# The head of a fused attention and mixture-of-experts kernel: order of the first loads, inverse roots of the first blocks on GpSimd, place of the router's centring, and the first slot tile's step

## The chip, the cores and the metric

The kernel runs on one core of one Trainium2 chip. A core has TensorE (PE, matrix products, with a weight load PEld ahead of each), VectorE (DVE), ScalarE (ACT), GpSimd (POOL) and SyncE (SP, which here only issues DMAs). Each engine works through its own instructions in order; they meet at semaphores. ScalarE, SyncE and GpSimd each have a queue for DMAs. The metric is the device time of one execution in microseconds.

## The reference

x is 4 sequences of 2048 rows of 256 numbers, all in float32.

```python
x = x + linear_attention(layernorm(x))     # 16 heads of 16
x = x + moe(layernorm(x))                  # 8 experts, 2 a row, 256 -> 512 -> 256
# linear attention, causal, with q, k = elu(...) + 1:
#   S_t = S_{t-1} + k_t v_t^T;  z_t = z_{t-1} + k_t
#   out_t = (q_t S_t) / (q_t z_t + 1e-6), then times Wo
# moe: logits = x router^T; the two largest, softmax over those two;
#   sum over them of p * (gelu(x w1 + b1) w2 + b2)
```

## The kernel before, in words

**Blocks.** The 8192 rows go through attention in 16 blocks of 512 rows (four tiles of 128). A block passes three stages, one a round of the main loop (L946): `stage_a` (L364: normalised rows transposed, keys, queries, running sum z of the keys, values with the router's eight columns, transposed keys, denominators), `stage_b` (L465: scores of each 128 rows, mask, products with the values, state), `stage_c` (L562: output projection px, x1 = x + attention, x1 stored to the output, choice of two experts, second normalising, slot of each row, and eight scatters L659 on GpSimd's queue that write each row twice to a table in DRAM, sorted by expert). In round s the loop runs stage a of block s, b of s-1 and c of s-2, a piece of each in turn.

**Slot tiles.** The table is worked off in 68 tiles of 256 rows of one expert (`slot_tiles`, L767), and up to four more under a condition. `plan` (L673) chooses the experts of a group of tiles (of 5, 4, 8, 8, 8, 8, 8 and 22) once the blocks that it needs are scattered. A tile is: fetch of its rows (L782, which waits for every scatter issued before it in the program), of w1 (L794), of w2 and b2 (L802, L806); `turned` (TensorE transposes, L815, copied by VectorE, L816); `hidden` (ph, L843, and Gelu on ScalarE); `output` (py, L860, plus b2 and weighted on VectorE, L865 and L869); and two indirect stores with addition into the output (L874, GpSimd's queue), each pair after the pair before it and after all x1 stores issued before it. The generator yields twice a tile: after hidden(j), turned(j+1) and the fetches of rows j+3 and w1 j+2; and after output(j-1), the store of an earlier tile and the fetch of w2 j+1. The main loop puts such steps between the pieces of attention by count (L955 to L972); ten steps are kept back for the last round, the rest follows when attention is over.

**Order.** SP's instructions stand in the order of the program (L108, written by hand). On the other engines a scheduler orders them by its own estimate of when they are ready. DMA semaphores are eight, handed out in turn, so a later DMA may have to wait for an earlier one that has the same semaphore.

**The head.** Block 0's rows come in four loads of 128 KB on ScalarE's queue (L120); the four 256 KB weights wk, wq, wv, wo on SP's (L131); then, on ScalarE's, the biases (L140 to L146), the router (L148) and b1 (L150). GpSimd builds the identity, masks and zeroed buffers (L154 to L217). `enter` (L354) normalises a block: statistics on VectorE (L271, L272), variance plus epsilon (L274), an inverse root by a bit trick and three Newton steps, eleven operations on 128x4 (L277 to L287), std and shift (L289, L292), then two of the four tiles normalised on VectorE (L302) and two on ScalarE (L297); GpSimd adds the output bias to x (L359). For blocks 1 to 5 it is called in stage a of the block before (L429); later blocks call it in their own stage a. `centre_router` (L318) takes the mean of the router's rows off (two matmuls with ones, two VectorE operations L326 that write eight columns beside wv); it is called in stage a of block 0, just ahead of the values.

Of the kernel before, what the change touches and what calls it, by code (L numbers as in the profile page):

```python
# [16 lines left out]
P = 128  # L17
# [7 lines left out]
def kernel(  # L25
# [89 lines left out]
    def load_x(n: int):  # L115
        b, s0 = blocks[n]
        xt = att.tile([P, NT, D], F32, tag="x", bufs=4, name=f"x_{n}")
        step = P if n == 0 else TB
        for i in range(0, TB, step):
            nc.scalar.dma_start(  # L120
                xt[:, i // P : (i + step) // P, :],
                x[b, s0 + i : s0 + i + step, :].rearrange("(t p) d -> p t d", p=P),
            )
        return xt
# [4 lines left out]
    def load_square(w, name, more=0):  # L129
        t = wpool.tile([P, NCC, D + more], F32, tag=name, name=name)  # L130
        nc.sync.dma_start(t[:, :, 0:D], w.rearrange("(cc p) o -> p cc o", p=P))  # L131
        return t

    wk_sb = load_square(wk, "wk_sb")
    wq_sb = load_square(wq, "wq_sb")

    wv_sb = load_square(wv, "wv_sb", E)
    wo_sb = load_square(wo, "wo_sb", E)
    bq_sb = const.tile([P, NCC], F32, tag="bq", name="bq_sb")
    nc.scalar.dma_start(bq_sb, bq)  # L140
    bk_sb = const.tile([P, NCC], F32, tag="bk", name="bk_sb")
    nc.scalar.dma_start(bk_sb, bk)
    bv_bc = const.tile([P, D], F32, tag="bv", name="bv_bc")
    nc.scalar.dma_start(bv_bc, bv.partition_broadcast(P))
    bo_bc = const.tile([P, D], F32, tag="bo", name="bo_bc")
    nc.scalar.dma_start(bo_bc, bo.partition_broadcast(P))  # L146
    rw_sb = const.tile([P, NCC, E], F32, tag="rw", name="rw_sb")
    nc.scalar.dma_start(rw_sb, rw.rearrange("(cc p) e -> p cc e", p=P))  # L148
    b1_sb = const.tile([P, E * NFC], F32, tag="b1", name="b1_sb")
    nc.scalar.dma_start(b1_sb, b1)  # L150
# [3 lines left out]
    make_identity(nc, ident)  # L154
    causal = const.tile([P, P], F32, tag="causal", name="causal")
# [68 lines left out]
    def ins_of(i):  # L224
        return getattr(i, "ins", i)

# [8 lines left out]

    def follow(inst, other):

        tc.add_manual_dep(
            ins_of(inst), ins_of(other).name,
            mybir.DependencyInfo(  # L240
                mybir.DependencyClass.NoSync, mybir.DependencyReason.SCHED_ONLY
            ), reason="order of issue",
        )
# [21 lines left out]

    def layernorm(src, dst, root_of=None):

        st = small.tile([P, NT, 6], F32, tag="st", name="st")
        mv = small.tile([P, NT, 2], F32, tag="mv", name="mv")
        for t in range(NT):  # L270
            nc.vector.bn_stats(st[:, t, :], src[:, t, :])  # L271
            nc.vector.bn_aggr(mv[:, t, :], st[:, t, :])  # L272
        rstd = small.tile([P, NT], F32, tag="rstd", name="rstd")
        nc.vector.tensor_scalar_add(rstd, mv[:, :, 1], LN_EPS)  # L274

        half = small.tile([P, NT], I32, tag="half", name="half")
        nc.vector.tensor_single_scalar(  # L277
            half, rstd.bitcast(I32), 1, op=ALU.logical_shift_right
        )
        guess = small.tile([P, NT], I32, tag="guess", name="guess")  # L280
        nc.vector.tensor_scalar(guess, half, -1.0, float(0x5F3759DF), ALU.mult, ALU.add)
        root = guess.bitcast(F32)
        error = small.tile([P, NT], F32, tag="error", name="error")
        for _ in range(3):
            nc.vector.scalar_tensor_tensor(error, root, -0.5, root, ALU.mult, ALU.mult)
            nc.vector.tensor_tensor(error, error, rstd, ALU.mult)
            nc.vector.scalar_tensor_tensor(root, error, 1.5, root, ALU.add, ALU.mult)  # L287
        if root_of is not None:
            nc.vector.tensor_tensor(root_of, rstd, root, ALU.mult)  # L289
        rstd = root  # L290
        shift = small.tile([P, NT], F32, tag="shift", name="shift")
        nc.vector.scalar_tensor_tensor(  # L292
            shift, mv[:, :, 0], -1.0, rstd, ALU.mult, ALU.mult
        )
        for t in range(NT):
            if t % 2:
                nc.scalar.activation(  # L297
                    dst[:, t, :], src[:, t, :], AF.Identity,
                    bias=shift[:, t : t + 1], scale=rstd[:, t : t + 1],
                )  # L300
                continue
            nc.vector.tensor_scalar(  # L302
                dst[:, t, :], src[:, t, :], mv[:, t, 0:1], rstd[:, t : t + 1],
                ALU.subtract, ALU.mult,
            )
        return rstd
# [45 lines left out]
    entered = {}  # L352

    def enter(n: int):  # L354
        xt = xs.pop(n)
        xn = att.tile([P, NT, D], F32, tag="xn", bufs=2, name=f"xn_{n}")
        std = small.tile([P, NT], F32, tag="std", bufs=3, name=f"std_{n}")
        layernorm(xt, xn, std)
        nc.gpsimd.tensor_tensor(  # L359
            xt, xt, bo_bc.unsqueeze(1).to_broadcast([P, NT, D]), ALU.add  # L360
        )
        entered[n] = xt, xn, std
# [668 lines left out]
```

## Time and profile before

| | |
|---|---|
| time, median of 3 runs | 1098.58 us (1096.32 to 1100.79) |
| profiled execution, its own time | 1100.39 us |
| its span, first to last instruction | 1098.5 us |
| mean granted TensorE clock | 0.968 |
| TensorE busy | 1005.2 us (92%) |
| VectorE busy | 763.7 us (70%) |
| ScalarE busy | 406.7 us (37%) |
| GpSimd busy | 387.0 us (35%) |
| chain that ended last, by engine | PE 69%, DVE 20%, DMA 6%, waiting for nothing shown 3% |

The profile is of one execution. A busy share is a mean over stretches with different limits, so it has to be read by stretch: which engine is full there, and what ended the idle time of the others. In timelines a row gives the start, the time taken, the engine, the line, the operation, output and inputs, the count, and in brackets the idle time before it with what ended that. A queue's name with a q (SPq, ACTq) marks an instruction that issues a DMA.

### The profile page before, as it was taken

What the parts mean: (1) busy time and instruction counts of PE and PEld (TensorE: products, weight loads), DVE (VectorE), ACT (ScalarE), POOL (GpSimd) and SP (SyncE); (2) the same over time, 40 slices, a digit from 0 to 9 for tenths busy, and PEclk for the clock granted to TensorE, in tenths of its full rate; (3) what the DMA queues carried; (4) which work ended last, traced back from release to release, by engine and by line L of the source; (5) the groups of instructions that cost most, each with busy time, mean ns of one, the idle gap of its engine ahead of it and who ended that gap; (6) DMA issues with size and microseconds to landing.
All of it is one profiled execution on the core that took longest, in us unless ns stands there. A gap on an engine that the chain in (4) does not pass through costs nothing.

```text
span 1098.5 us, 23167 instructions
## 1 busy us (share of the span) xinstructions
PE 1005.2 (92%) x8358; PEld 802.0 (73%) x8358; DVE 763.7 (70%) x2665; ACT 406.7 (37%) x842; POOL 387.0 (35%) x302
## 2 busy tenths in 40 slices
PE   4998888789998999999999999999999879999991
PEld 2666565576767787878787877788788768888880
DVE  8877989769797769795979688767776713343320
ACT  3543343424452535353535344363532112222220
POOL 4003123022342424435353525153325343444344
PEclk9998998889999999999999999999999989999996
DMA  6001123342525474655647382837374588999853
GB/s 213 1 21 60 42 68 119 113 145 49 175 49 175 92 217 97 189 136 151 178 102 220 76 251 59 233 60 215 82 217 107 159 247 231 227 238 242 229 129 39
DMA packets 128724, 155.23 MB, mean 141 GB/s; under 512 B 9952, under 2 KB 105952, under 8 KB 128608
## 3 DMA queue, kind: packets, MB, share of 16 engines
q1 hardware_dynamic: 84944, 101.78, 29.4%
q0 software_dynamic: 25728, 34.88, 17.3%
q10 hardware_dynamic: 17936, 17.07, 4.9%
q8 instruction: 67, 1.10, 0.4%
q14 instruction: 49, 0.40, 0.1%
HBM read 108.05 MB, written 45.65 MB: 140 GB/s over the span
## 4 chain that ended last, share of the span: by engine, by line
PE 69%; DVE 20%; DMA 6%; issue 3%; POOL 1%; ACT 1%; ACTq 0%; POOLq 0%; SPq 0%; DVEq 0%
PE py L860 19%; PE ph L843 18%; PE pp L381 6%; PE pn L514 5%; DMA out_dram<-y,to 5%; PE sc L486 4%; DVE at L491 4%; PE pv L406 4%; PE px L574 4%; PE pn L507 3%; PE pt_xs L815 2%; DVE st L271 2%; DVE z L391 2%; PE pt_xn L263 1%; PE pk L425 1%
## 5 line engine op out<-in xcount | busy, mean ns | idle before, releaser
L874 POOL DMA_INDIRECT out_dram<-y,to x136 | 216.6, 1592 | 459.4 <-DVE y L869 112.9
L843 PE MATMUL ph<-xT,w 128*128 128x256 f32 x1088 | 253.8, 387 | 13.4 <-DMA w<-in_w_dram 7.6
L860 PE MATMUL py<-w,hT 128*128 128x256 f32 x1088 | 250.9, 384 | 0.0
L843 PEld LDWEIGHTS ph<-xT,w 128*128 128x128 f32 x1088 | 208.6, 194 | 45.5 <-issue 15.6
L860 PEld LDWEIGHTS py<-w,hT 128*128 128x128 f32 x1088 | 202.8, 191 | 32.8 <-issue 4.7
L849 ACT ACTIVATE hT<-ph,b1t 128x256 f32<-128x256 f32 x272 | 112.4, 471 | 301.5 <-PE ph L843 261.5
L491 DVE TENSOR_TENSOR at<-sc,causal 128x512 f32<-128x512 f32 x256 | 158.4, 682 | 8.9 <-PE sc L486 8.9
L659 POOL DMA_INDIRECT rows<-xn,slots x128 | 124.5, 973 | 49.4 <-issue 33.2
L865 DVE TENSOR_TENSOR y<-py,b 128x512 f32<-128x512 f32 x68 | 46.9, 690 | 124.2 <-PE py L860 124.2
L816 DVE COPY xT<-pt_xs 128x512 f32<-128x512 f32 x68 | 46.8, 689 | 98.8 <-PE pt_xs L815 98.8
L359 POOL TENSOR_TENSOR x<-x,bo_bc 128x1024 f32<-128x1024 f32 x16 | 37.8, 2361 | 196.6 <-ACT xn L297 138.4
L477 ACT ACTIVATE qM<-qs,parity 128x256 f32<-128x256 f32 x128 | 56.3, 499 | 93.2 <-DVE qs L456 44.2
L486 PE MATMUL sc<-qM,kT 32*128 32x256 f32 x1024 | 76.0, 401 | 5.7 <-ACT share L416 5.3
L514 PE MATMUL pn<-at,vpad 128*32 128x128 f32 x2048 | 74.0, 288 | 0.0
L486 PEld LDWEIGHTS sc<-qM,kT 32*128 32x128 f32 x1024 | 47.6, 184 | 32.0 <-issue 16.9
L406 PE MATMUL pv<-wv_sb,xnT 128*128 128x264 f32 x256 | 62.9, 399 | 8.6 <-DVE wv_sb L326 4.8
L514 PEld LDWEIGHTS pn<-at,vpad 128*32 128x32 f32 x2048 | 55.3, 115 | 8.8 <-issue 1.1
L406 PEld LDWEIGHTS pv<-wv_sb,xnT 128*128 128x128 f32 x256 | 48.4, 195 | 17.8 <-DVE wv_sb L326 4.9
L574 PE MATMUL px<-wo_sb,vT 128*128 128x264 f32 x256 | 61.1, 392 | 0.0
L869 DVE TENSOR_SCALAR y<-y,wt 128x256 f32<-128x256 f32 x136 | 58.5, 472 | 1.9
L381 PE MATMUL pp<-xnT,wk_sb 128*128 128x512 f32 x128 | 59.6, 609 | 0.2 <-ACT xnT L264 0.2
L381 PE MATMUL pp<-xnT,wq_sb 128*128 128x512 f32 x128 | 58.2, 597 | 0.0
(163 smaller groups left out, 1288.1 us busy)
## 6 DMA issues: line engine op xcount, KB each, us to landing
w<-in_w_dram SPq DMA_DIRECT2D x136, 512.0 KB, 5.7
xs<-rows SPq DMA_DIRECT2D x68, 260.0 KB, 3.3
b<-in_b_dram SPq DMA_DIRECT2D x68, 128.0 KB, 5.8
out_dram<-x ACTq DMA_DIRECT2D x16, 512.0 KB, 4.5
x<-in_x_dram ACTq DMA_DIRECT2D x15, 512.0 KB, 4.3
rows<-none SPq DMA_DIRECT2D x1, 2340.0 KB, 9.4
out_dram<-y,to POOLq DMA_INDIRECT x136, 3.9
rows<-xn,slots POOLq DMA_INDIRECT x128, 2.5
```

The lines of the kernel that those rows point to most:

```text
L381: nc.tensor.matmul(pp, w[:, cc, ts(m, P)], xnT[:, cc, :], start=(cc == 0), stop=(cc == NCC - 1),)
L406: nc.tensor.matmul(pv, xnT[:, cc, ts(t, P)], wv_sb[:, cc, :], start=(cc == 0), stop=(cc == NCC - 1),)
L486: nc.tensor.matmul(sc[g][:, m, :, :], kT[part, m, ts(c, P)], qM[part, m, :, :], start=True, stop=True,)
L491: nc.vector.tensor_tensor(at[:, g].rearrange("p m r i -> p (m r) i"), sc[g].rearrange("p m r i -> p (m r) i"), causal.unsqueeze(1).to_broa ...
L514: nc.tensor.matmul(pn[W * g : W * g + W, m, :], vp[:, c, NG * m + g, W * par : W * par + W], at[:, g, m, par, :], start=False, stop=(par = ...
L574: nc.tensor.matmul(px, vT[:, cc, ts(t, P)], wo_sb[:, cc, :], start=(cc == 0), stop=(cc == NCC - 1),)
L659: s = ins_of(nc.gpsimd.indirect_dma_start(out=rows[:, :], out_offset=bass.IndirectOffsetOnAxis(ap=slots[:, 2 * t + k : 2 * t + k + 1], axi ...
L843: nc.tensor.matmul(ph[:, i, :], w1t[:, cc, ts(f, P)], xT[:, cc, :], start=(cc == 0), stop=(cc == NCC - 1),)
L849: nc.scalar.activation(hT[:, f, :], ph[:, i, :], AF.Gelu, bias=bias[:, f : f + 1])
L860: nc.tensor.matmul(py[:, a, :], hT[:, f, ts(a, P)], w2t[:, f, :], start=(f == 0), stop=(f == NFC - 1),)
L869: nc.vector.tensor_scalar_mul(yt[:, a, :], yt[:, a, :], wt[:, a : a + 1])
L874: i = ins_of(nc.gpsimd.indirect_dma_start(out=out_rows, in_=yt[:, a, :], in_offset=None, compute_op=ALU.add, bounds_check=T - 1, oob_is_er ...
```

## The change

Five things change.

- **First loads.** Block 0's four loads are shared out, the first and third on SP's queue, the others on ScalarE's, ahead of all else. ScalarE's queue then has the router and wk; SP's has bk, wq, bq, wv, bv, bo, wo, b1.
- **Early normalising.** `layernorm` and `enter` move ahead of the masks, and block 0 enters there, right behind the identity.
- **Roots on GpSimd.** For blocks 0 to 5 the eleven operations are replaced by one GpSimd power, (variance + epsilon) to -0.5, on 128x4. For these blocks the statistics are also ordered behind the last block's shift or z*q on VectorE (an order of issue, not a wait). Later blocks, and the second normalising of all blocks, keep the Newton steps.
- **Router.** It is centred right behind block 0's transposes.
- **First slot tile.** A yield is put between turned(0) and the loop, so that hidden(0) and all behind it come one step later. The conditional tiles (one at a time) are left as they are.

```diff
-            nc.scalar.dma_start(
+            (nc.sync if n == 0 and i // P % 2 == 0 else nc.scalar).dma_start(
                 xt[:, i // P : (i + step) // P, :],
...
-    wk_sb = load_square(wk, "wk_sb")
-    wq_sb = load_square(wq, "wq_sb")
-
-    wv_sb = load_square(wv, "wv_sb", E)
-    wo_sb = load_square(wo, "wo_sb", E)
...
     nc.scalar.dma_start(rw_sb, rw.rearrange("(cc p) e -> p cc e", p=P))
+    wk_sb = load_square(wk, "wk_sb", nc.scalar)
+    bk_sb = const.tile([P, NCC], F32, tag="bk", name="bk_sb")
+    nc.sync.dma_start(bk_sb, bk)
+    wq_sb = load_square(wq, "wq_sb", nc.sync)
...
+    wv_sb = load_square(wv, "wv_sb", nc.sync, E)
...
+    wo_sb = load_square(wo, "wo_sb", nc.sync, E)
...
     make_identity(nc, ident)
+    neghalf = const.tile([P, NT], F32, tag="neghalf", name="neghalf")
+    nc.vector.memset(neghalf, -0.5)
...
+    QUIET = ROUND_ENDS[0] + 2
+
+    def layernorm(src, dst, root_of=None, power=False, behind=None):
...
+        for t in range(NT):
+            i = nc.vector.bn_stats(st[:, t, :], src[:, t, :])
+            if behind:
+                follow(i, behind[0])
+            nc.vector.bn_aggr(mv[:, t, :], st[:, t, :])
+        rstd = small.tile([P, NT], F32, tag="rstd", name="rstd")
+        nc.vector.tensor_scalar_add(rstd, mv[:, :, 1], LN_EPS)
+        if power:
+            root = small.tile([P, NT], F32, tag="root", name="root")
+            nc.gpsimd.tensor_tensor(root, rstd, neghalf, ALU.pow)
+        else:
...
+        i = nc.vector.scalar_tensor_tensor(
+            shift, mv[:, :, 0], -1.0, rstd, ALU.mult, ALU.mult
+        )
+        if behind is not None:
+            behind[:] = [i]
...
+    entered = {}
+    turn = []
+
+    def enter(n: int):
...
+        layernorm(xt, xn, std, n <= QUIET, turn if n <= QUIET else None)
...
+    enter(0)
+
     causal = const.tile([P, P], F32, tag="causal", name="causal")
...
         transposed(xn, xnT, "xn")
+        if n == 0:
+            centre_router()
         yield
...
-        nc.vector.tensor_tensor(z, z, qT, ALU.mult)
+        i = nc.vector.tensor_tensor(z, z, qT, ALU.mult)
+        if n > 0:
+            turn[:] = [i]
         vp = vpads[n % 2]
...
-        if n == 0:
-            centre_router()
...
-        if n < ROUND_ENDS[0] + 2:
+        if n < QUIET:
 
             enter(n + 1)
...
         turned(0)
+        if J > 1:
+            yield
         wait = []
```

## The prediction

> **What bounds the kernel now.** I read the slices of the page first, then the busy times by window, then TensorE's and GpSimd's timelines, the chain of waits, and last the order of instructions in both built programs.
>
> ```profile
> PE   4998888789998999999999999999999879999991
> DVE  8877989769797769795979688767776713343320
> ```
> TensorE (first row) is full from slice 14 on (27.5 us each) except at slices 32, 33 and the end; time can be won only in the head, near 860 to 890 us, and in the tail. The windows (length, then busy us of PE, weight loads, VectorE, ScalarE, GpSimd, granted clock, DMA share, GB/s):
>
> ```profile
> 80.00:100.00 20.00, 16.38 (x186) 11.80 (x188) 19.62 (x64) 7.47 (x17) 5.12 (x4) 0.98 0.13 41
> 120.00:140.00 20.00, 14.70 (x247) 11.41 (x245) 19.55 (x68) 6.54 (x17) 5.90 (x5) 1.00 0.14 47
> 160.00:180.00 20.00, 13.01 (x169) 9.83 (x171) 19.48 (x73) 6.44 (x17) 7.95 (x7) 0.86 0.18 61
> 500.00:600.00 100.00, 99.97 (x942) 80.55 (x942) 79.98 (x292) 42.57 (x87) 38.55 (x29) 1.00 0.62 175
> ```
> Where TensorE idles early (3.6, 5.3 and 7.0 us in these rows), VectorE is full (97 to 98%): it is the bound there. From 400 to 850 us TensorE is, and a gain made before passes through unchanged.
>
> ```profile
> 27.75 5.45 PE L406 MATMUL pv<-wv_sb,xnT 128*128 128x264 f32 x16 [4.77 <-DVE wv_sb L326]
> 200.13 6.16 PE L843 MATMUL ph<-xT,w 128*128 128x256 f32 x16 [5.79 <-issue]
> 891.92 6.71 PE L843 MATMUL ph<-xT,w 128*128 128x256 f32 x16 [7.58 <-DMA w<-in_w_dram]
> ```
> Three single stalls (in brackets): the values wait for the centred router; the first slot tile waits for its turned rows, which VectorE copies at 199.33; a tile after the last block waits for its w1.
>
> ```profile
> 870.93 1.61 POOL L874 DMA_INDIRECT out_dram<-y,to  x1 [16.72 <-DVE y L869]
> ...
> 884.97 1.62 POOL L874 DMA_INDIRECT out_dram<-y,to  x1 [0.30 <-issue]
> ...
> 1089.73 1.55 POOL L874 DMA_INDIRECT out_dram<-y,to  x1 [3.00 <-DMA out_dram<-y,to]
> ```
> The tail is a chain of stores. From 884.97 (just behind the last block's eight scatters) to 1089.73 there are 28 pairs, each waiting for the pair before to land: 204.8/27 = 7.58 us a pair. TensorE needs 7.35 us a tile and its last tile is weighted at 1075.9, 13.8 us before its store is issued. So the end follows the last scatter, not TensorE.
>
> **The start: 6 us.** Now the last quarter of x reaches VectorE at 6.86, the roots end at 10.85, the transposes start at 11.47, and z*q, which the denominators need, ends at 31.48. After: x's quarters lead both queues, issued at 0.83 and 1.30 (an issue takes 0.47), and the weights no longer share with them. The first quarter now lands 2.9 us after its issue, so the last would at about 4.2; four statistics of 0.43 from 3.7 on end at 5.4, the variances at 5.8. But behind ScalarE's x and wk stand three 512 KB loads ahead of its table load and its half of the normalising. The built program gives DMAs eight semaphores in turn; so the third load waits for the first to land. The first is issued when x's first quarter has landed (about 3.5) and needs 4.3 us (median of these loads) to 5 with the weights beside it: about 8.2. Then an issue 0.45, table load 1.28, two normalisations 1.2: 11.1 instead of 12.14. So TensorE starts only 1 us sooner; VectorE's earlier roots are hidden by ScalarE.
>
> GpSimd now takes the root between its mask builds, so these come later: from about 6.6 us it has 4.4 us of builds (by their rows: 0.29, 0.20, 0.30, 0.34, 0.50, 0.33, 0.50, 0.17, 1.79), then x0+bo (2.34) from 11.1, when ScalarE is done with x, then 3.44 (0.50, 1.79, 0.50, 0.52, 0.13), so that block 1's root comes at about 17.1. From that VectorE's order gives kT of block 0 at 18.4 (now 20.47); one scan still waits out GpSimd's x1+bo (the scan at 21.22 took 3.35 against 1.22, beside that addition). Without block 2's statistics and Newton steps in between, z*q ends near 27.8. The router's two operations now precede kT, so the values no longer wait until 27.75 and TensorE has done them and the key transposes by then; pd goes from 34.0 to 27.9. Gain 6; bounds 3 (loads of 6.5 us) and 8 (x1+bo collides with nothing).
>
> **The roots: 4 us.** Per block 11 small operations leave VectorE (half, guess, nine Newton steps), 0.16 to 0.17 us each at a pitch of 0.195: 2.15 us. A GpSimd power of 128x4 comes in; the trace has none. Nearest rows: the 128x4 IOTA, 0.13 us, and the 128x1024 addition, 2.36. Size says the first, work per element more: I take 0.3, and 0.2 for both hand-overs. VectorE's next instruction is the one that waits, and kT, z and the score masks queue behind it; so 1.6 us net a block. Blocks 2 to 5 lie in the stretch above: 6.6 us, of which TensorE gets what falls in VectorE-bound windows; two thirds, 4. Bounds: 0, and 13 (all, and two half-clock stretches go):
>
> ```profile
> 85.00:99.40 14.40, 10.78 (x128) 7.95 (x126) 14.02 (x47) 4.94 (x13) 4.53 (x4) 1.00 0.15 46
> 99.40:106.20 6.80, 6.25 (x105) 5.56 (x105) 2.64 (x7) 2.33 (x6) 5.28 (x6) 0.50 0.31 110
> ```
> After gaps of at most 1.36 us the granted clock halves for 6.8 us (3.4 us of work lost); again at 174.5 and 198.4. [...]
>
> [...]
>
> **The first slot tile: 6 us.** Its transposes stay, but the hidden layer now follows pp (3.6), pn, PV and one more set of scores, some 10 us of work, while VectorE does its copy. Gone are the 5.79 idle and 6.16 - 3.72 = 2.44 us of half clock: 8.2. Late next: pn, for the masks that VectorE ends at 199.3, with pp done at 197.9: 1.4 to 2 back. Bounds 8 and 0 (VectorE, busy 17.9 of 20 us at 180 to 200, is simply late elsewhere).
>
> **Order from 220 to 850: 0.** Hidden and output layers swap places; nothing is added, SP's fetches keep their order, and the same tiles wait for the same scatters, save the last. TensorE has 12.3 us of stalls from 226 to 335 behind VectorE, which may move: plus or minus 4.
>
> **The tail: 6 us.** With one step more ahead, every tile stands half a tile later against attention. The last block's px comes one hidden layer (3.65 + 0.4) sooner, and the last scatter and its 28 pairs with it: 4. Second, the store that scatter stands behind waits for the last block's x1 to land, which took 9.3 us (median 4.5) beside two groups of tile loads. Now tile 44, not 45, is first to wait for the last scatter (SP is in order, w1 and w2 queue behind it), so only one group is in flight: up to 4.8 sooner, I take 4. Against that: TensorE has one output layer less to do before tile 43's w1 comes, and one tile (7.35) more after; its 13.8 us lead over the stores falls to about 6, and one or two more pairs run beside loads (7.6 instead of 6.4 us): 2 back. Bounds 9 and -4.
>
> **Sum.** 6 + 4 + 6 + 0 + 6 = 22. The profiled execution took 1100.39 (span 1098.5 and 1.9 around it): 1078.4. The median of the runs, 1098.58, lies 1.8 lower, inside their spread; I say 1078.
>
> **Rivals.**
> - VectorE stays the bound to 240 us: roots and first tile give back nearly all (VectorE at 97% speaks for it, removed VectorE work against), start and tail hold: 1100.4 - 11 = 1089.
> - The moved order does not do what it says: ScalarE held by the third load (start 2), the relief outside the bound windows (0), the first tile late on VectorE (2), and the x1 landing as slow as now (tail 0): 1096, no change that a measurement can tell. For it: each is a bound above; against: all at once.
> - Slower: the power is long. VectorE waits for it in order, in six blocks. With first tile and tail keeping 12, it costs 6 x (p - 2.2); it is slower by 5.5 from p = 5.1 us, and at p = 6 gives 1111. Against: every computing row of GpSimd is under 2.4 us, for 256 times the elements.
>
> **Chances.** Forecast 0.62 (1066 to 1085), first rival 0.22, second 0.10, third 0.04, the rest 0.02. The range takes in the first rival and the bounds of the terms: 1066 to 1093. About 0.5% (5.5 us) is what a measurement of this kernel can tell from no change: faster 0.86, same 0.09, slower 0.05.
>
> **What would show it.** Right: transposes near 10.5 and pd near 28 us; a power row under 0.5 us; no idle before the first ph; TensorE's windows at 80 to 180 with under 10 us of idle; the last px some 20 us sooner, x1's landing near 5 us, stores still the last chain. Wrong: ScalarE's table load behind 10 us; VectorE idle on the power; new idle between 345 and 850; TensorE, not the stores, last in the chain.

## The result, and the profile after

| | before | after |
|---|---|---|
| time, median of 22 runs each | 1099.55 us (1094.14 to 1105.12) | 1095.81 us (1087.98 to 1104.28) |
| profiled execution, its own time | 1100.39 us | 1100.47 us |
| its span | 1098.5 us | 1098.6 us |
| mean granted TensorE clock | 0.968 | 0.955 |
| TensorE busy / idle in the span | 1005.2 / 93.3 us | 1021.7 / 76.9 us |

The ratio after to before is 0.9956 [0.9938, 0.9975]; the medians lie 3.7 us apart. Forecast were 22 us; the time lies above the whole range, and within 0.5% of no change. The profiled execution of after is one of its slower ones, 4.7 us above its own median, so the two traces end alike.

The slices of the page of after: TensorE, VectorE, and the granted clock in tenths.

```profile
PE   5897987989999999999999999999999879999993
...
DVE  7768878879597959796888789786776733333331
...
PEclk9878888989999999999999999999999989999997
```
The clock row of the page of before:

```profile
PEclk9998998889999999999999999999999989999996
```
Over the early slices together (20 to 345 us) TensorE is busier, 286.4 us against 279.2, and the granted clock is lower, 0.88 against 0.94. 16.4 us of idle time went, and 16.5 us of busy time came: the same multiplications took longer. Half-clock time over the whole span went from 70.7 to 99.9 us, which is 14.6 us of work. By window, after (columns as in the prediction):

```profile
80.00:100.00 20.00, 17.34 (x176) 11.43 (x174) 19.86 (x67) 10.76 (x23) 2.26 (x2) 1.00 0.14 47
120.00:140.00 20.00, 17.92 (x184) 12.91 (x184) 17.79 (x48) 8.57 (x20) 2.24 (x2) 0.83 0.10 27
160.00:180.00 20.00, 15.97 (x159) 10.85 (x161) 17.82 (x62) 9.68 (x21) 1.04 (x1) 0.99 0.14 47
500.00:600.00 100.00, 100.00 (x906) 81.79 (x905) 78.72 (x289) 37.34 (x83) 37.26 (x29) 1.00 0.58 156
```
TensorE's idle time in the three early rows fell from 15.9 to 8.8 us, but at 120 to 140 part of the busy time ran at half clock. The three single stalls and the stores, in the timelines of after:

```profile
21.25 3.72 PE L426 MATMUL pv<-wv_sb,xnT 128*128 128x264 f32 x16
...
219.57 5.41 PE L863 MATMUL ph<-xT,w 128*128 128x256 f32 x16
...
892.04 5.78 PE L863 MATMUL ph<-xT,w 128*128 128x256 f32 x16 [5.98 <-DMA w<-in_w_dram]
```
```profile
871.35 1.57 POOL L894 DMA_INDIRECT out_dram<-y,to  x1 [9.79 <-DVE ed L634]
...
885.28 1.61 POOL L894 DMA_INDIRECT out_dram<-y,to  x1 [0.30 <-issue]
...
1090.01 1.55 POOL L894 DMA_INDIRECT out_dram<-y,to  x1 [3.10 <-DMA out_dram<-y,to]
```
The stall before the values and the one before the first hidden layer are gone, as forecast, though the first hidden layer still takes 5.41 us, part of it at half clock, where 3.72 were counted on; the w1 stall lost 1.6 us. The stores begin and end where they did.

Milestones of the two profiled executions (us; block in brackets), where each stage starts on TensorE:

| | pr(0) | pd(1) | pr(1) | px(0) | pr(2) | px(2) | px(4) | px(15) | last row scatter | last store |
|---|---|---|---|---|---|---|---|---|---|---|
| before | 36.3 | 56.5 | 58.7 | 70.4 | 97.6 | 144.7 | 243.6 | 856.5 | 883.7 | 1091.6 |
| after | 31.4 | 54.7 | 57.8 | 71.7 | 102.4 | 153.7 | 245.1 | 861.7 | 884.0 | 1091.9 |
| difference | -5.0 | -1.8 | -0.9 | +1.3 | +4.8 | +9.0 | +1.5 | +5.2 | +0.3 | +0.3 |

The head wins 5.0 us, all of it is lost again by px(0), and the blocks behind lose more. From pr(0) to px(0), before:

```profile
36.34:70.38 34.04, 31.31 (x410) 22.21 (x411) 25.42 (x47) 17.44 (x38) 1.98 (x1) 1.00 0.01 2
```
and after:

```profile
31.35:71.67 40.32, 37.69 (x410) 27.02 (x411) 28.11 (x60) 18.65 (x40) 3.37 (x2) 0.84 0.01 2
```
The same 410 multiplications take 6.4 us more, at a clock of 0.84; TensorE idles 2.7 and 2.6 us, and VectorE is busy for 75% and 70% only. So in this stretch the lead is lost to half clock, and not to waiting. From px(0) to px(3) TensorE idles 17.8 and 18.6 us, and 11.5 and 35.7 us of its busy time run at half clock. (At px(4) before has one output layer of 3.6 us more behind it.) The last px was forecast some 20 us sooner and comes 5 later; only between it and the last scatter are 4.9 us won back.

### The profile page after: what moved, and what is told of

The parts are those of the page before. It is cut to its first block, busy times and chain, and to the rows that moved or that the text cites. A ratio compares the mean times of both kernels' runs of the same rounds, so it can differ in the third digit from the quotient of the medians.

```text
span 1098.6 us, 23082 instructions
## 1 busy us (share of the span) xinstructions
PE 1021.7 (93%) x8358; PEld 816.1 (74%) x8358; DVE 769.5 (70%) x2600; ACT 385.7 (35%) x824; POOL 394.1 (36%) x308
## 4 chain that ended last, share of the span: by engine, by line
PE 68%; DVE 20%; DMA 4%; issue 2%; POOL 1%; ACT 1%; SPq 0%; POOLq 0%; DVEq 0%
PE ph L863 20%; PE py L880 18%; PE pn L534 5%; DVE at L511 5%; PE pp L401 4%; PE sc L506 4%; PE px L594 3%; PE pv L426 3%; DMA out_dram<-y,to 3%; PE pn L527 3%; PE pt_xs L835 2%; DVE st L179 2%; DVE z L411 2%; PE pr L471 1%; PE pt_xn L335 1%
## 5 line engine op out<-in xcount | busy, mean ns | idle before, releaser
L880 PE MATMUL py<-w,hT 128*128 128x256 f32 x1088 | 248.0, 381 | 0.0
L506 PE MATMUL sc<-qM,kT 32*128 32x256 f32 x1024 | 80.4, 413 | 5.3 <-ACT share L436 5.3
L534 PE MATMUL pn<-at,vpad 128*32 128x128 f32 x2048 | 77.0, 296 | 0.0
L506 PEld LDWEIGHTS sc<-qM,kT 32*128 32x128 f32 x1024 | 50.1, 190 | 30.6 <-issue 7.3
L541 ACT COPY vT<-pn 128x256 f32<-128x256 f32 x64 | 23.7, 371 | 129.9 <-PE pn L534 126.2
L594 PE MATMUL px<-wo_sb,vT 128*128 128x264 f32 x256 | 63.8, 404 | 0.0
L594 PEld LDWEIGHTS px<-wo_sb,vT 128*128 128x128 f32 x256 | 49.2, 197 | 12.6 <-issue 3.5
L232 POOL TENSOR_TENSOR x<-x,bo_bc 128x1024 f32<-128x1024 f32 x16 | 42.0, 2625 | 44.9 <-ACT xn L213 37.6
```

The costliest lines, as they stand in the source:

```text
L506: nc.tensor.matmul(sc[g][:, m, :, :], kT[part, m, ts(c, P)], qM[part, m, :, :], start=True, stop=True,)
L534: nc.tensor.matmul(pn[W * g : W * g + W, m, :], vp[:, c, NG * m + g, W * par : W * par + W], at[:, g, m, par, :], start=False, stop=(par = ...
L594: nc.tensor.matmul(px, vT[:, cc, ts(t, P)], wo_sb[:, cc, :], start=(cc == 0), stop=(cc == NCC - 1),)
L880: nc.tensor.matmul(py[:, a, :], hT[:, f, ts(a, P)], w2t[:, f, :], start=(f == 0), stop=(f == NFC - 1),)
```

## The experiments

Three theories stood against each other. **Clock:** the gain goes back because shorter, more spread stalls halve TensorE's clock more often. **Wait:** VectorE, in order, waits for the power and does the next block's layernorm ahead of masks and denominators. **Addition**: the power pushes GpSimd's x+bo (the output bias added to x) to where it holds up VectorE.

**Two kinds of chip.** The kernel before took 1099.6 and 1101.5 us on two of the chips, and 1172 to 1180 on four others, where TensorE stands still beside GpSimd's row scatters (last section). A ratio holds for its kind of chip; kernels measured side by side share a letter below. The same kernel on two chips of the second kind came out 0.3 to 0.4% apart (1.0232 and 1.0274, 1.0224 and 1.0252, 1.0265 and 1.0291), so across letters less than 0.4% says nothing. e7 is a single execution of the kernel before on chip b, 1172.4 us. A ratio here is not the quotient of two medians (1095.81/1099.55 would be 0.9966). Before the first scatter (about 97 us) the traces of both kinds can be compared.

| kernel | chip | median us | ratio to before |
|---|---|---|---|
| after (first measurement) | first kind | 1095.81 | 0.9956 [0.9938, 0.9975] |
| turn alone (e1) | second, a | 1206.71 | 1.0232 [1.0200, 1.0263] |
| change with Newton (e2) | second, a | 1206.75 | 1.0224 [1.0192, 1.0256] |
| change without the turn (e3) | second, a | 1185.16 | 1.0039 [1.0015, 1.0064] |
| change without the order (e4) | second, a | 1212.58 | 1.0257 [1.0222, 1.0292] |
| after (e5) | second, b | 1213.75 | 1.0315 [1.0279, 1.0351] |
| after, stalls filled too long (e6) | second, b | 1222.84 | 1.0408 [1.0367, 1.0449] |
| addition later (e8) | second, c | 1209.35 | 1.0265 [1.0234, 1.0295] |
| Newton, no turn (e9) | second, c | 1178.47 | 1.0003 [0.9982, 1.0024] |
| power alone (e10) | second, c | 1183.80 | 1.0043 [1.0021, 1.0065] |
| after, stalls filled shorter (e11) | second, c | 1209.47 | 1.0270 [1.0241, 1.0299] |
| loads and router alone (e12) | first kind, d | 1098.79 | 1.0004 [0.9969, 1.0038] |
| Newton, no turn, filled (e13) | first kind, d | 1095.55 | 0.9950 [0.9921, 0.9978] |
| addition later, no turn (e14) | first kind, d | 1095.72 | 0.9970 [0.9937, 1.0003] |
| the same, filled (e15) | first kind, d | 1097.23 | 0.9973 [0.9935, 1.0010] |
| turn alone (e16) | second, e | 1203.80 | 1.0274 [1.0240, 1.0309] |
| addition later, with the turn (e17) | second, e | 1206.20 | 1.0291 [1.0253, 1.0329] |
| change with Newton (e18) | second, e | 1201.83 | 1.0252 [1.0215, 1.0290] |

### The power: Newton in its place, and the power alone

```diff
-        layernorm(xt, xn, std, n <= QUIET, turn if n <= QUIET else None)
+        layernorm(xt, xn, std, False, turn if n <= QUIET else None)
```


> The change with the root on VectorE (Newton) in all blocks again; loads, router, order and slot tile as in after. Theory 1: TensorE still halves its clock in many short stretches, because the stalls stay short and spread; 1094 to 1100 against the 1095.8 of after, half-clock time before 345 us 60 to 90 us. Theory 2: without the 1.1 us wait for the power the masks come sooner or no later; 1088 to 1092. The prediction's own term for the roots says the opposite, 4 us worse than after: 1100.

> The whole change with Newton's steps in place of the power, once more, for such a chip: the roots term there. The prediction: 4 us slower than the changed kernel, 0.999. From the first runs (power 4 to 10 us dearer than Newton): 0.988 to 0.992. On a chip like the first three: 1.0224 again.

The other way round, the power for the first six blocks of the kernel before:

> The kernel before with the power on GpSimd for the first six blocks, and nothing else of the change. The prediction's term: 4 us faster, ratio 0.996. Theory 2 and theory 3: 3 to 9 us slower, 1.003 to 1.008; theory 3 adds that the loss shows as an instruction of some 2 us, in place of 0.2, on VectorE in front of rden in blocks 2 to 4, theory 2 that it shows as 1.1 us waits for the power with the masks behind them.

The power costs, on this kind of chip: alone it is 0.43% slower (c), where the prediction had 0.4% faster. Newton in its place is 0.6 to 0.9% better than after (e and a against b), and without the turn 0.36% better (e9 against e3, across letters, so no more than two chips differ by). In the profiled runs px(15) came at 949.9 with the power alone and at 941.1 in the kernel before on such a chip (e7).

In these two profiles most of the loss stands already in the head: with the power alone pr(0) comes 5.6 us later than in e7, px(0) 6.0 and px(15) 8.8. GpSimd and VectorE in e10:

```profile
19.56 2.36 POOL L366 TENSOR_TENSOR x<-x,bo_bc 128x1024 f32<-128x1024 f32 x1 [2.44 <-ACT xn L304]
21.87 1.03 POOL L281 TENSOR_TENSOR root<-rstd,neghalf 128x4 f32<-128x4 f32 x1
```
```profile
22.93 2.30 DVE L296 TENSOR_TENSOR std<-rstd,root 128x4 f32<-128x4 f32 x1 [3.99 <-POOL root L281]
```
Block 2's root stands behind block 0's addition on GpSimd. VectorE waits 3.99 us for it, the instruction that waited then takes 2.30 (0.16 elsewhere) beside the next addition, and kT of block 0 comes at 27.67 in place of 20.69. Later three more small VectorE instructions take 2.0 to 2.3 us beside an addition, ahead of masks and denominators (98.00, 146.16, 192.54), as the third theory expected, while the waits for the power there are 0.1, 0 and 0.9 us. In after the order of issue keeps block 2's statistics out of the head, and the power costs in another way. Two things in VectorE's timeline of after show how:

```profile
51.86 0.17 DVE L184 TENSOR_SCALAR rstd<-mv 128x4 f32<-128x4 f32 x1
53.16 0.16 DVE L203 TENSOR_TENSOR std<-rstd,root 128x4 f32<-128x4 f32 x1 [1.13 <-POOL root L187]
...
53.96 2.48 DVE L511 TENSOR_TENSOR at<-sc,causal 128x512 f32<-128x512 f32 x4
...
99.05 2.08 DVE L675 CAST slots<-slot_f 128x8 uint32<-128x8 f32 x1
101.04 0.28 DVE L463 TENSOR_SCALAR rden<-pd 128x128 f32<-128x128 f32 x1
```
VectorE waits 1.13 us for the power with the masks queued behind it. And a conversion of 128x8 numbers takes 2.08 us, in front of the denominators. GpSimd at that time, in after:

```profile
94.98 1.02 POOL L187 TENSOR_TENSOR root<-rstd,neghalf 128x4 f32<-128x4 f32 x1 [37.66 <-DVE rstd L184]
98.76 2.34 POOL L232 TENSOR_TENSOR x<-x,bo_bc 128x1024 f32<-128x1024 f32 x1 [2.77 <-ACT xn L213]
```
and the same two instructions in before, on GpSimd and on VectorE:

```profile
92.79 2.38 POOL L359 TENSOR_TENSOR x<-x,bo_bc 128x1024 f32<-128x1024 f32 x1 [54.47 <-ACT xn L297]
```
```profile
92.25 2.48 DVE L491 TENSOR_TENSOR at<-sc,causal 128x512 f32<-128x512 f32 x4
...
96.18 0.17 DVE L655 CAST slots<-slot_f 128x8 uint32<-128x8 f32 x1
```
In before the addition lies beside the four masks, which read PSUM and take 2.48 us for four beside it as they do elsewhere. In after it starts 6 us later, and the conversion beside it ends when it does, at 101.1. The same happens at 139.11 and 180.90 (2.09 and 2.08 us, a copy of 128x8).

### GpSimd's addition moved

```diff
-        nc.gpsimd.tensor_tensor(
+        i = nc.gpsimd.tensor_tensor(
             xt, xt, bo_bc.unsqueeze(1).to_broadcast([P, NT, D]), ALU.add
         )
+        if 2 < n <= QUIET:
+            follow(i, scattered[-1])
...
+                scattered[:] = [d]
```
Three additions go behind eight scatters each; nothing else moves on any engine.

> The change with one thing moved: GpSimd's addition x+bo of blocks 3, 4 and 5 stands behind the row scatters of two blocks earlier, no longer in front of them; the order on the other engines is the same as in the changed kernel. A third theory, from the traces of before and after: that addition takes 2.34 us, and a small VectorE instruction that falls beside it takes about 2.08 us where the same one takes 0.17 elsewhere. With the power ahead of it on GpSimd the addition starts at 98.76 and meets the slot arithmetic in front of rden (99.05, 139.11, 180.90: one instruction of 2.08 us in each of blocks 2, 3, 4), where before it lay at 92.79 beside the masks, which kept their 0.62 each. Theory 3 expects: the three 2.08 us are gone from in front of rden, pr(2) comes about 2 us sooner (101.6 in place of 103.6 in the run of the changed kernel), TensorE's stalls before pr of blocks 2 to 4 fall from 3.6, 2.6 and 2.3 to about 1.6, 0.6 and 0.3, the half-clock stretches behind them too, and the time by 4 to 8 us against the changed kernel (ratio to before 1.024 to 1.028 where that one gave 1.0315, 0.988 to 0.992 where it gave 0.996). Theory 2 (the wait for the power itself) expects the stalls to stay, within 2 us of the changed kernel.

GpSimd, VectorE and TensorE in that run:

```profile
93.06 1.02 POOL L187 TENSOR_TENSOR root<-rstd,neghalf 128x4 f32<-128x4 f32 x1 [34.60 <-DVE rstd L184]
98.24 1.20 POOL L682 DMA_INDIRECT rows<-xn,slots  x1 [4.17 <-issue]
...
108.36 2.35 POOL L233 TENSOR_TENSOR x<-x,bo_bc 128x1024 f32<-128x1024 f32 x1
```
```profile
97.13 0.17 DVE L678 CAST slots<-slot_f 128x8 uint32<-128x8 f32 x1
```
```profile
98.54 1.76 PE L474 MATMUL pr<-rden,spread 32*128 32x128 f32 x16 [1.74 <-DVE rden L467]
```
All three instructions of 2.08 us are gone, the conversion takes 0.17, and TensorE's stall before pr(2) is 1.74 us in place of 3.65 in e5. pr(2) starts 5.1 us sooner and px(15) at 974.8 against 980.6. So the collision is real, it stands on the path, and the moved addition removes it. It goes with the power: all seven traces with the power and the addition where it was (after, e3, e4, e5, e6, e10, e11) have three small VectorE instructions of 2.0 to 2.3 us between 90 and 200 us, and of the thirteen others only e13 has one that long. On the whole time the step is 0.5% (c against b), hardly more than the chips differ by.

> The change with GpSimd's addition behind the scatters (as in the run where that was the one thing moved) and without the turn. The change without the turn gave 1.0039, with Newton in place of the power 1.0003. Theory 3 (what the power costs is the addition that it pushes beside the slot arithmetic): 0.998 to 1.000, as good as Newton or better. Theory 2 (the wait for the power has its own price): between the two, 1.001 to 1.003.

0.9970 on the first kind: a little better than expected. Up to px(3) no slot tile has begun in either, and e14 and after have the same instructions in the same order but for these three additions: e14 is there at 188.6 us, after at 197.7, so on the first kind too, by these two profiles, the moved addition wins 9.1 us there. With the turn, on the second kind:

> The whole change with GpSimd's addition behind the scatters, once more, for such a chip: without the turn it gave 0.997 there, the changed kernel 0.9956. If the turn is worth its 5 us and the moved addition 3 to 6: 0.990 to 0.993, the best version of all. If the two overlap: 0.995 to 0.997. On a chip like the first three: 1.0265 again.

1.0291, and Newton beside it 1.0252 (intervals that overlap); px(15) came at 968.6 and 968.2. With the addition out of the way the power is about as good as eleven small operations, and not the 4 us better of the prediction.

### The head: loads and router, with and without the order

> Loads, router and order of issue alone: the change without the power (Newton in all blocks) and without the turn in the slot tiles. Theory 2 and theory 3 alike (the power costs, by its wait or by what it pushes): 5 to 9 us better than the change without the turn alone, ratio to before 0.994 to 0.999 where that one gave 1.0039. The prediction's terms: start 6, so 0.995. Theory 1 alone (any removed stall goes back through the clock): 1.000 to 1.004.

1.0003: nothing is left of the head's gain. This kernel and the kernel before (e7) on TensorE, before the first scatter; first the kernel before:

> The kernel before itself, one profile on the same chip as the two others. On a chip like the first: about 1099, half-clock stretches before 345 us 30 to 60 us. On the second chip: about 1180, and stalls without a releaser in the hidden layers' blocks, as in the other four runs.

```profile
36.58 0.73 PE L451 MATMUL pr<-rden,spread 32*128 32x128 f32 x16 [0.62 <-DVE rden L444]
...
56.78 0.62 PE L437 MATMUL pd<-z,heads 128*32 128x128 f32 x16
...
58.89 1.16 PE L451 MATMUL pr<-rden,spread 32*128 32x128 f32 x16 [0.42 <-DVE rden L444]
...
63.43 1.08 PE L514 MATMUL pn<-at,vpad 128*32 128x128 f32 x32
```
then loads, router and order:

```profile
30.47 0.73 PE L471 MATMUL pr<-rden,spread 32*128 32x128 f32 x16 [0.62 <-DVE rden L464]
...
52.41 0.65 PE L457 MATMUL pd<-z,heads 128*32 128x128 f32 x16 [0.41 <-DVE at L511]
...
57.26 1.16 PE L471 MATMUL pr<-rden,spread 32*128 32x128 f32 x16 [1.92 <-DVE rden L464]
...
62.83 1.94 PE L534 MATMUL pn<-at,vpad 128*32 128x128 f32 x32
```
6.1 us ahead at pr(0), 4.4 at pd(1), 1.6 at pr(1), 0.8 behind at px(0). The stall before pr(1) is the next block's layernorm: with the order its statistics, Newton steps and two halves (47.9 to 55.9) stand in front of rden on VectorE, where the kernel before does them later. It grows from 0.42 to 1.92 us, and two half-clock stretches (31.7 and 59.0) take most of the rest: the pn at 62.83 took 1.94 us, the one at 63.43 in the first fence 1.08.

> Loads and the router's place alone: no power, no order of issue, no turn. In the run with the order (Newton, no turn) pr(0) came 6.1 us sooner than in the kernel before and px(1) no sooner (115.0 against 114.9): 0.9 us went to a half-clock stretch at 31.7, about 3 to the next block's layernorm in front of rden of block 1, 2.5 to half clock at 59.0. If the order is what saves the start: pr(0) back at about 36 (the statistics of block 1 in front of z*q again) and the time at 1.000 to 1.003. If the order only moves the loss into block 1: pr(1) sooner than 57.3 and ratio 0.996 to 0.999. The prediction put the start at 6 (0.995) and the order at 0.

Without the order pr(0) is back at 36.9 (on the first kind), pr(1) at 60.8, and the time is 1.0004. The order saves the start and then pays for it in block 1.

> The change without the order of issue that puts the next block's statistics behind the product z*q; the power stays on GpSimd. Theory 1: other places for the stalls, the same clock loss: 1094 to 1100. Theory 2: the statistics go back into VectorE's gaps ahead of the masks, the 1.2 us before pd and the 3.6 us before pr(2) go: 1089 to 1092. The prediction put this part at 0.

Here pr(0) came at 38.1, and the time at 1.0257 was no worse than after in e5. Without the order the addition does not meet the slot arithmetic (the conversion took at most 0.37 us), but it meets other small instructions, ahead of the masks: they take 2.32, 2.02 and 2.14 us, at 94.19, 144.36 and 190.94. So the collision comes with the power, with the order and without it; the order only sets which instruction it hits.

### The stalls filled: is it the clock?

The clock records of all twenty traces, cut into the stretches of 3.41 us that the records themselves mark (in before and in after every change of the granted clock lies a whole number of them behind the first): a stretch at full clock is followed by another in some 5500 cases, none of them with more than 2.01 us of TensorE idle, and by one at half clock in 365; of these 365 the least idle was 0.67 us, the middle one 2.18, and 154 had 2.01 or less. Full clock comes back only behind a halved stretch with at most 0.72 us idle. Two such places in after (windows as above):

```profile
97.50:101.00 3.50, 1.21 (x24) 0.72 (x16) 3.43 (x8) 1.35 (x3) 2.24 (x1) 0.99 0.00 0
101.00:107.80 6.80, 5.00 (x68) 4.25 (x68) 5.31 (x12) 2.08 (x5) 5.13 (x6) 0.50 0.23 81
128.30:131.70 3.40, 1.62 (x14) 0.84 (x16) 3.12 (x7) 1.06 (x5) 0.00 (x0) 1.00 0.55 157
131.70:138.50 6.80, 6.50 (x46) 5.01 (x45) 5.54 (x21) 2.65 (x7) 1.04 (x1) 0.50 0.01 2
```
So whether a stall of about 2 us halves the clock can depend on where it falls in the stretches. In these records a stretch idle for part of its length is enough (more than 2.01 us in every case, 0.67 to 2.01 in 154), so stalls of 1.4 to 2 us can matter. Half-clock time before 345 us was 37 us in the profile of before (not 51, as the expectation of e1 has it) and 75 in that of after. To see whether it costs time, idle multiplications keep TensorE busy in its stalls (they write what the next real one overwrites):

```diff
+        fill(prs[0], FILL_PR.get(n, 0))
...
+        for _ in range(k):
+            nc.tensor.matmul(
+                dst, ident, wk_sb[:, 0, 0:w], start=True, stop=True, skip_group_check=True
+            )
```


> The changed kernel itself once more, to stand beside the others on one chip. The four runs before this one were on a chip on which the kernel before took 1179.5 us and TensorE stood still in places for which the profile shows no releaser (39.7 us before state_ps in the run with the turn alone), so their times are read against the changed kernel on the same chip. If this is that chip: 1200 to 1210, since the turn alone cost 2.3% there. If it is one like the first: 1094 to 1097, ratio 0.996.

> The change with idle multiplications in TensorE's stalls in front of pd (blocks 0 and 1), pr (blocks 2 to 7) and pn (second group of blocks 2 and 3), 68 in all and each group about as long as the stall it stands in; they write to the PSUM tile that the next real multiplication overwrites. In the profiles of before and after a stretch of 3.41 us in which TensorE stood still for 1.75 us or more is followed by one at half clock in every case but none with less than 0.77. Theory 1 (the gain went back through the clock): the half-clock stretches before 345 us fall from 75 us to 20 to 40, and the time by 6 to 12 us against the changed kernel, ratio to it 0.989 to 0.995. Theory 2 (VectorE is the bound in these stages, TensorE only arrives earlier and waits longer): the clock rises too, but the time stays within 2 us of the changed kernel.

1.0408, slower by 9 us: each took 0.46 us, twice my figure, and stood longer than the stall (6.2 us before pr(4)). Half as many:

> The change with idle multiplications in TensorE's stalls once more, half as many: in the run before they took 0.46 us each at 256 columns and not 0.23, so that they were longer than the stalls (6.2 us in front of pr of block 4). Now 6, 4, 3, 1, 2 and 3 of them in front of pr of blocks 2 to 7, 1 and 3 in front of pn of blocks 2 and 3, 7 and 3 narrower ones in front of pd of blocks 0 and 1. Theory 1: half-clock stretches before 345 us at most 45 us against the 75 to 95 of the changed kernel, and 5 to 10 us faster than it (ratio to before 1.023 to 1.027 where it gave 1.0315). If the stalls are VectorE's and TensorE would only wait longer: the clock higher, the time within 2 us of the changed kernel.

1.0270 against 1.0315: as forecast in size, but across chips, and half-clock time before 345 us was 55 us (89 in e5), above the 45 that the clock theory allowed. Then side by side on the first kind of chip:

> The run with loads, router and order alone (ratio 1.0003), with idle multiplications in its stalls: 3, 3, 5, 2 and 3 in front of pr of blocks 1 to 5, 1 and 1 in front of pn of blocks 2 and 3. Theory 1 (what is gained at the start goes back through the clock): the half-clock stretch at 59.0 goes, px(0) comes at 68 to 69 in place of 71.4, and the time falls by 4 to 8 us, ratio 0.993 to 0.997. If VectorE is the bound: px(0) at 71 and 0.999 to 1.002.

> The run before this one with idle multiplications in its stalls: 7 and 3 narrow ones in front of pd of blocks 0 and 1, 3, 2, 1 and 2 in front of pr of blocks 2 to 5, 1 and 3 in front of pn of blocks 2 and 3. The version that the runs so far point to: power, no collision, no long stall. Theory 1: 5 to 8 us better than without them, ratio 0.992 to 0.996. If the clock costs nothing because VectorE is the bound: within 2 us of the run without them.

The unfilled and the filled kernel, 20 to 345 us (PE, PEld, DVE, ACT, POOL busy, clock, DMA share, GB/s), e14:

```profile
20.00:345.00 325.00, 284.24 (x2859) 210.24 (x2861) 262.73 (x882) 131.83 (x278) 82.41 (x68) 0.91 0.28 85
```
and e15:

```profile
20.00:345.00 325.00, 285.83 (x2916) 210.67 (x2915) 264.62 (x888) 132.86 (x281) 82.43 (x68) 0.95 0.29 88
```
The clock rises from 0.91 to 0.95, half-clock time falls from 58 to 34 us, px(2) comes 4.4 us sooner, but px(6) only 1.6 and px(15) 1.5; the time is 1097.2 against 1095.7 us: no gain. It takes two stretches to read this. From pr(0) to px(0), e14:

```profile
31.70:73.30 41.60, 38.82 (x411) 27.89 (x411) 28.07 (x60) 18.65 (x40) 3.37 (x2) 0.82 0.01 2
```
and e15:

```profile
32.50:70.00 37.50, 34.21 (x417) 24.38 (x417) 27.85 (x60) 18.51 (x40) 3.38 (x2) 0.95 0.01 2
```
Here the filling shortens the stretch by 4 us, so here the clock is what costs. From px(0) to px(3) the two take 115.3 and 114.6 us: 6.0 us less of work went to half clock, but idle time and idle multiplications together rose from 15.4 to 21.0 us. TensorE came sooner and waited longer. Over the runs of one kernel time and clock do go together (-0.89 over the 22 runs of after, 8.5 us for 0.01), but longer stalls lower the clock (above 2.01 us in a stretch, every time) and lengthen the time alike. So the clock takes the head's lead in the first block; behind px(0) it is not borne out as the cause. These are single profiles. e13 has no unfilled twin on this kind of chip, so its 0.9950 does not tell the filling from the rest; the half-clock stretch at 59.0 was gone there, but px(0) came at 71.2, not at the 68 to 69 of the clock theory.

### The turn in the slot tiles

```diff
         turned(0)
+        if J > 1:
+            yield
```


> The kernel before with the one added turn in the slot tiles, and nothing else of the change. Theory 1 (the early stages give their gain back to TensorE's clock): this part is worth by itself what the trace of after shows at the end, the milestones from px(15) to the last pair, about 5 us: 1094 to 1095, ratio 0.995; half-clock stretches before 345 us stay near the 51 us of before. Theory 2 (VectorE waits in order for the power and does the layernorm ahead of the masks): the same 0.995. Rival to both, that the tail's 5 us is only the early stages' delay made up again (px(15) was 5.2 us late in after because one hidden layer more was still to do): ratio 1.000.

> The kernel before with the added turn alone, once more, for a chip on which TensorE does not stand still beside the scatters (the last four runs were on one: before 1101.5 there, no stall without a releaser between the scatters). The prediction's term: 6 us, ratio 0.9945. From the traces of before and after the tail gave 4.9: 0.9955. If the turn's gain at the end is only work that the blocks' stages then lack: 0.999 to 1.001. On a chip like those of the first three calls: 1.023 again.

> The change without the added turn in the slot tiles. Theory 1 and theory 2 alike: the 5 us of the tail are lost, 1100 to 1101, ratio 1.000 to 1.002, the early part alone being worth nothing as the run of after stands. Prediction's terms (start 6, roots 4): 1089. Rival that the tail's gain is only a delay made up: 1096.

On the second kind of chip the turn costs 2.3 to 2.7%, and without it the change is at 1.0039. TensorE's waits (line, what ended them; us, times, longest), the kernel before (e7):

```profile
PE state_ps L525 <- issue: 16.3, 30, 1.2
...
PE ph L843 <- issue: 7.0, 4, 5.8
```
and with the turn alone (e16):

```profile
PE state_ps L525 <- issue: 34.7, 49, 1.2
...
PE pk L425 <- issue: 10.0, 19, 1.2
```
How the turn costs this is not shown. It shifts the layers against the blocks, and more runs of very small multiplications (state_ps, pk) stall; but all stalls without a releaser together make 45.5 us in e7 and 49.4 in e16, while the two executions lie 27.5 us apart. Half-clock time goes from 125 to 170 us, which is 22.6 us of work; what makes it so is open. On the first kind of chip, where those stalls are absent, the turn was not measured alone. There only two readings of it stand: the stall of 5.79 us before the first hidden layer is gone, and from px(15) to the last scatter after needs 22.3 us, the kernel before 27.2, and the four kernels without the turn 25.3 to 26.1 (e12 to e15). That is 3 to 5 us at the end of attention. Its cause stands in the traces: in all six the store in front of the last scatters starts 0.8 us after the last block's x1 has landed, and that landing took 9.3 us in before, 6.4 to 8.1 in e12 to e15 and 4.5 in after. That store of x1 (L580 in before, L600 in after), first before:

```profile
DMA to landing us min/median/max: 9.3/9.3/9.3
```
then after:

```profile
DMA to landing us min/median/max: 4.5/4.5/4.5
```

## Why the prediction was wrong, point by point

Of the 22 us some 4 came. Two steps failed: the 5 us won at the start did not pass through (TensorE lost 6.2 us to half clock by px(0)), and the roots term had the wrong sign (the waits for the power and three additions that hold up VectorE). Of the tail one part of two came, and the worth of the first slot tile is open.

- **Start, 6 us.** The working held: pd at 28.3 (27.9 forecast), kT at 19.1 (18.4), the scan beside x1+bo 3.4 us, pr(0) 5.0 us sooner. What failed is the step from there into the sum. "A gain made before passes through unchanged" was said of 400 to 850 us. The lead was gone at px(0), one block later: 12.4 us of TensorE's busy time up to there ran at half clock, none in before, which is 6.2 us of work. The sum took the clock as it was; its windows begin at 80 us and leave out the stretch from 30 to 72, where TensorE and not VectorE is nearly full. e9 shows the same (6.1 us ahead at pr(0), 0.8 behind at px(0), ratio 1.0003), and without the order of issue the lead never stood (e12: pr(0) at 36.9, 1.0004).
- **Roots, 4 us.** This step failed with its sign, measured on the second kind of chip. Three parts of it: the power takes 1.02 to 1.04 us (0.3 taken; the two rows named, 0.13 and 2.36, held it), VectorE waits 0.8 to 1.2 for it in order instead of 0.5, in five blocks of six; and GpSimd's addition, which starts only when ScalarE has read x, comes later and beside the slot arithmetic, three times 2 us in front of the denominators; with the addition moved px(3) comes 9.1 us sooner (e14). The prediction priced this very collision once (x1+bo beside a scan, 3.35 against 1.22) and did not ask where the additions of blocks 2 to 5 would go. Measured: 0.4% lost alone (most of it by another wait, in the head), about even when the addition is moved.
- **First slot tile, 6 us.** The stall of 5.79 us went; of the 2.44 us of half clock in the layer itself only 0.75 did. What it was worth on the first kind of chip is open.
- **Order, 0 ± 4.** px(2) to px(15) stand 1.5 to 12.6 us later; this takes up what the three terms above promised. The statement that the swap is free held on the first kind only (345 to 850 full in both traces), and cost over 2% on the second.
- **Tail, 6 us.** Its second part came: the last block's x1 landed 4.8 us sooner (4 taken, 4.8 at most), and the time from the last px to the last scatter fell by 4.9. The first did not show: the last px, forecast one hidden layer sooner, came 5.2 us later, behind blocks that were late already. Behind the last scatter, every kernel here has 28 pairs of stores; from that scatter to the last store the six traces of the first kind took 200.7 (e12) to 207.9 us, and before and after 207.9 both. So this chain, the same code in all, moves the end by 7 us from one execution to another; in the profiles of before and after it took the same, and the end follows the last scatter: 883.7 and 884.0.
- **Clock.** The upper bound of the roots counted on half-clock stretches going; they doubled (37 to 75 us). Filling took 24 us of half clock away (e14 to e15); it won 4 us in the first block and no time in all.
- **Rivals.** The first (VectorE stays the bound, 1089) named the right bound for the stretch behind px(0), but let the start through. The second gave 1096, the measured time, for wrong reasons: ScalarE was not held (table load at 9.2 us), the first tile was not late, the last x1 landed in 4.5 us in place of 9.3. The third: p is 1.04 us, far below 5.1.
- **Signs.** Four signs of being right came (pd at 28.3, no idle before the first ph, 8.8 us of idle in the three windows, the x1 landing at 4.5), but not the one that sums them up, the last px 20 us sooner; of those of being wrong, VectorE's idle time on the power came.
- **Still open:** the turn alone on the first kind of chip; how the turn costs over 2% on the second; how the cost of the power in the changed kernel splits between its wait and the addition; why the lead of e15 over e14 fades between px(3) and px(6).

No version tried beats the changed kernel on the first kind of chip by more than the intervals (0.9950 against 0.9956), and none beats the kernel before on the second (best 1.0003).

## What to carry to other kernels

Carry a gain forward only to the next place where its engine is the bound: the 5 us at pr(0) were real, and gone 40 us later, because TensorE, nearly full there, ran at half clock for part of the way (a clock of 0.84 there against 1.00 in before); behind that VectorE was the bound. So ask of a lead what clock the next stretch will have. When an instruction moves off an engine, list what stands behind it on the engine that receives it, and ask beside what each of those will now run: here the waits for the power and the additions that came later for it cost more than the eleven operations a block that it saved (the power alone: 1.0043). And measure at a milestone (the last scatter) and over many executions: with a chain behind it that varies by 7 us, one pair of profiles could not have shown a change of 4.

## What the runs showed of the hardware

- **The large GpSimd addition held up some VectorE work.** Beside x+bo (2.34 us) one VectorE instruction of 128x8 took 2.08 us in place of 0.17 and ended with the addition. Not all work is held: beside such additions in after a reduction of 128x64 kept its 0.22 us, a reciprocal of 128x128 its 0.95, and masks that take one input from PSUM theirs (2.48 us for four). What sets the held instructions apart is not shown. Moving the addition removed it (0.17 in e8).
- **A power of 128x4 on GpSimd takes 1.02 us** in after, some seven times the 128x4 iota there (0.14; 0.13 in before); the first one took 1.04.
- **On the second kind of chip TensorE stood still, and a product of it was taken up late, while GpSimd issued scatters.** In the kernel before (e7) 82 stalls without a releaser make 45.5 us, 34.2 of them beside the row scatters; on the first kind the same kernel has a single one, the 5.79 us before the first hidden layer, which e7 has too. The late product, on TensorE and VectorE in the run with the addition moved (e8):

```profile
103.09 0.44 PE L548 MATMUL state_ps<-vpad,k_tok 128*32 128x32 f32 x16
```
```profile
109.90 0.42 DVE L559 TENSOR_TENSOR S<-state_ps,own 128x256 f32<-128x256 f32 x1 [7.76 <-remote]
```
VectorE starts 6.4 us after the product that it needs has ended, while eight scatters are issued (98.24 to 108.33); on the first kind TensorE waits 0.55 us for the same S. Up to pr(2) the two profiles of the kernel before stand together (97.6 and 97.8 us), at the last scatter they are 78.5 us apart, and the stores behind take no longer (207.9 and 201.5). So the kernel's 7% between the chips arises while there are scatters; the stalls on TensorE are half of it, and the rest is not split. Why the chips differ, no run here tells.
